# Second mixture of experts: every batch scatters its tokens to the experts' places itself, and an expert reads its places with one plain transfer

## The chip, the core and the metric

The kernel runs on one core of a Trainium2 chip. The core has five engines that run on their own and wait for each other through semaphores: PE (TensorE, matrix products and transposes), DVE (VectorE, elementwise work and reductions), ACT (ScalarE, activation functions and copies), POOL (GpSimd, elementwise work and the indirect transfers) and SP (SyncE, which issues the plain transfers). Transfers between DRAM and the on-chip memory run on 16 DMA engines. The metric is the time of one execution on the device in microseconds (us); lower is better.

## The reference, cut to what matters

Four layers of cross-attention and a feed-forward part work on `x`, 4 batches of 512 tokens of 128 numbers, in float32. All eight parts are residual: `x = x + part(layernorm(x))`. The change is in the feed-forward part of the third layer, a mixture of 8 experts of which every token uses two:

```python
logits = xf @ w_g                                  # 2048 tokens x 8 experts
topv, topi = jax.lax.top_k(logits, 2)
probs = softmax over the two
capacity = int(2 * 1.25 * 2048 / 8)                # 640 places for each expert
mask = one_hot(topi.T, 8)                          # first choices of all tokens, then second ones
rank = cumsum(mask.reshape(2 * 2048, 8), axis=0).reshape(2, 2048, 8) - 1
mask = mask * (rank < capacity)
...
h = gelu(einsum("ecd,edh->ech", exp_batches, c_fc))      # 640 x 128 by 128 x 512
exp_out = einsum("ech,ehd->ecd", h, c_proj)              # 640 x 512 by 512 x 128
out = einsum("nec,ecd->nd", cb, exp_out)                 # weighted with probs
```

First choices have precedence: a token's second choice is ranked behind the first choices of all 2048 tokens. A choice that finds no place is dropped.

## The kernel before

Tokens lie on the 128 partitions: batch `g` is a tile `X[g]` of 128 partitions by 4 (`NJ`) by 128 numbers, so there are 16 (`NT`) tiles of 128 tokens. The text is written with generators that yield between steps; `together` (L117) runs several of them in turn, one step each. A framework then puts the instructions on the engines' queues in an order of its own and adds the semaphore waits, also those for buffers that are used again. Each engine works through its queue in order.

The parts that matter here, in order of time:

- The second layer's feed-forward part `l1_ffn` (L923) ends with `write(g)` (L1053) for each batch: POOL makes masked keys (`block_keys`, L262), PE folds them (L1056), and attention over 16 slots follows. It is queued, batch by batch, with `after(g)`, the third layer's attention `attend2(g)` and `route2(g)`; `together` runs all four batches in step (L1064).
- `attend_few` (L430) is that attention. It scales the softmax terms on POOL (L449).
- `routed` (L558) normalises a batch into a tile `xn` (L230), stores it to the DRAM table `xd2` (L567, SP), transposes it on PE with some filler matmuls ahead (L89, `ident` by `ident`, results unused), and multiplies with the router's weights (L571). DVE copies the logits (L577).
- `l2_ffn` (L1090) starts when all logits are there. DVE finds both choices of all tokens (`argmax`, L586). `places` (L604) turns them into ranks with matrix products. `tokens_of_slots` (L627) turns "which place has this token" into "which token has this place" (L644 to L683): comparisons on DVE (L644, L655), 32 matmuls (L659), and a few small operations give `inv`, the token of each place, and `to`, the row of the result table `yd2` to which each place's result goes. Both are 128 by 5 (`NCH2`) by 8 experts.
- The experts: each has 640 places, that is five chunks of 128, treated as a group of three and a group of two (L1111). For each chunk POOL issues an indirect gather of 128 rows from `xd2` (L765), 40 in all. PE transposes a group (L797), DVE copies it (`exT`, L798), PE multiplies with the first weights (L1125), ACT applies gelu (L1128), PE multiplies with the second weights (L1133), DVE copies the result (`ye`, L1140), and POOL scatters it to `yd2`, one indirect transfer for each chunk (L774), 40 in all. Gathers and scatters share POOL's queue. Between the experts the weights of the fourth layer's attention are prepared (L315, L334, L349, L291).
- `combine` (L1148): SP reads `yd2` plainly (L1153), and DVE adds both choices' results, weighted, to `x` (L1159). It needs all scatters. The fourth layer follows.

The first mixture (L802) has gathers and scatters of the same kind, 8 of each, on the same two lines.

The expert weights `f2w1` and `f2w2` (L1335, L1336) are fetched during `l1_ffn`. The result table's first 4096 rows are set to zero early on (L1276), by eight SP transfers.

Of the kernel before, what the change touches and what calls it, by code (L numbers as in the profile page):

```python
# [16 lines left out]
P = 128  # L17
# [30 lines left out]
        ("tile", 2 * NT), ("row", 1), ("spare0", NEXP), ("spare2", NCH2 * NEXP), ("chunks", NCH2), ("ctxT", 128)]  # L48
# [19 lines left out]
def tile_kernel(ctx: ExitStack, tc: tile.TileContext, I, out):  # L68
# [146 lines left out]
    def normed(src, tag, plus=0.0, act=False, p=P, n=NJ, bufs=B, pool=wk):  # L215

        mv, r = yield from moments(src, p, n)
        y = pool.tile([P, n, D], F32, tag=tag, name=tag, bufs=bufs)
# [211 lines left out]
    def attend_few(g, keys, vw, H, scores_bias):  # L430
# [18 lines left out]
        nc.gpsimd.tensor_tensor(e3, e3, bc(rec, 2, M), ALU.mult)  # L449
# [108 lines left out]
    def routed(tag, w, bias=None, copies=(), fill=0):  # L558
# [5 lines left out]
        def chain(g):  # L564
            xn[g] = yield from normed(X[g], "xn")
# [38 lines left out]
    def places(ohs):  # L604

        sums, found = [], []
        for k, oh in enumerate(ohs):
            oh2 = oh.rearrange("p t e -> p (t e)")
            pt = psum()
            nc.tensor.matmul(pt[:, :P], lhsT=oh2, rhs=ones, start=True, stop=True)  # L610
            cs = rt.tile([P, P], BF16, tag="cs", name="cs", bufs=2)
            nc.scalar.copy(cs, pt[:, :P])
            sums.append(cs)
            pt = psum()
            nc.tensor.matmul(pt[:, :P], lhsT=tri, rhs=oh2, start=True, stop=False)
            for k0 in range(k):
                nc.tensor.matmul(pt[:, :P], lhsT=sums[k0], rhs=same, start=False, stop=False)
            nc.tensor.matmul(pt[:, :P], lhsT=cs, rhs=before, start=False, stop=True)
            own = rt.tile([P, NT, NEXP], F32, tag="own", name="own")
            nc.vector.tensor_tensor(own.rearrange("p t e -> p (t e)"), oh2, pt[:, :P], ALU.mult)  # L620
            rank = rt.tile([P, NT], F32, tag="rank", name="rank", bufs=2)
            nc.vector.tensor_reduce(rank, own, AX.X, ALU.add)
            nc.vector.tensor_scalar(rank, rank, -1.0, None, ALU.add)
            found.append(rank)
        return found

    def tokens_of_slots(ohs, ranks, cap, spare):  # L627

        nch = cap // P
        pt = psum()
        for k, (oh, rank) in enumerate(zip(ohs, ranks)):
            ri = rt.tile([P, NT], I32, tag="ri", name="ri", bufs=2)
            nc.vector.tensor_copy(ri, rank)
            nc.vector.tensor_scalar(ri, ri, P - 1, None, ALU.bitwise_and)
            lo = rt.tile([P, NT], BF16, tag="lo", name="lo", bufs=2)
            nc.vector.tensor_copy(lo, ri)  # L640
            Rs = []
            for t0 in range(0, NT, NJ):
                R = wk.tile([P, NJ, P], BF16, tag="aT", name="R", bufs=B)
                nc.vector.tensor_tensor(R, bc(iota, 1, NJ), bc(lo[:, t0 : t0 + NJ], 2, P), ALU.is_equal)  # L644
                Rs.append(R)
                if t0 == 0:
                    hi = rt.tile([P, NT], F32, tag="hi", name="hi", bufs=2)
                    nc.vector.tensor_tensor(hi, rank, lo, ALU.subtract)
                    in_ = rt.tile([P, NT, nch], BF16, tag="in", name="in_", bufs=2)
                    nc.vector.tensor_tensor(in_, bc(hi, 2, nch), bc(C["chunks"][:, :nch], 1, NT), ALU.is_equal)  # L650
                    tk = rt.tile([P, NT, 2, NEXP], BF16, tag="tk", name="tk", bufs=2)
                    nc.vector.tensor_scalar(tk[:, :, 0, :], oh, C["row"], None, ALU.mult)
                    nc.vector.tensor_tensor(tk[:, :, 1, :], oh, bc(C["tile"][:, k * NT : (k + 1) * NT], 2, NEXP), ALU.mult)
                    th = rt.tile([P, NT, nch, 2 * NEXP], BF16, tag="th", name="th", bufs=2)
                    nc.vector.tensor_tensor(  # L655
                        th, bc(tk.rearrange("p t i e -> p t (i e)"), 2, nch), bc(in_, 3, 2 * NEXP), ALU.mult
                    )
            for t in range(NT):
                nc.tensor.matmul(  # L659
                    pt[:, : nch * 2 * NEXP],  # L660
                    lhsT=Rs[t // NJ][:, t % NJ, :],
                    rhs=th[:, t].rearrange("p c e -> p (c e)"),
                    start=k == 0 and t == 0,
                    stop=k == len(ohs) - 1 and t == NT - 1,
                )
        inv = rt.tile([P, nch, NEXP], I32, tag="inv", name="inv")
        got = rt.tile([P, nch, 2, NEXP], F32, tag="got", name="got")
        nc.vector.tensor_copy(got.rearrange("p c i e -> p (c i e)"), pt[:, : nch * 2 * NEXP])
        token = rt.tile([P, nch, NEXP], F32, tag="token", name="token")
        nc.vector.scalar_tensor_tensor(token, got[:, :, 1, :], float(P), got[:, :, 0, :], ALU.mult, ALU.add)  # L670
        row = rt.tile([P, nch, NEXP], F32, tag="row", name="row")
        nc.vector.tensor_scalar(row, token, -1.0, 0.0, ALU.add, ALU.max)
        if len(ohs) > 1:
            again = rt.tile([P, nch, NEXP], F32, tag="again", name="again")
            nc.vector.tensor_scalar(again, row, float(NTOK), float(-NTOK), ALU.is_ge, ALU.mult)
            nc.vector.tensor_tensor(inv, row, again, ALU.add)
        else:
            nc.vector.tensor_copy(inv, row)
        to = rt.tile([P, nch, NEXP], I32, tag="to", name="to")
        none = rt.tile([P, nch, NEXP], F32, tag="none", name="none")  # L680
        nc.vector.tensor_scalar(none, token, 0.0, None, ALU.is_equal)
        nc.vector.tensor_tensor(none, none, spare.rearrange("p (c e) -> p c e", c=nch), ALU.mult)
        nc.vector.tensor_tensor(to, row, none, ALU.add)  # L683
        return inv, to
# [183 lines left out]
    def l1_xattn(keys, vw):  # L868
        def chain(g):

            def scores_bias(dst, src, r):
                for j in range(NJ):
                    s = slice(j * 2 * M, (j + 1) * 2 * M)
                    nc.vector.scalar_tensor_tensor(
                        dst[:, s].rearrange("p (h n) -> p h n", h=2),
                        src[:, j, :].rearrange("p (h n) -> p h n", h=2),
                        r[:, j : j + 1],
                        bc(bias1[:, g * NJ + j, :], 1, 2),
                        ALU.mult,
                        ALU.add,  # L880
                    )

            return attend_few(g, keys, vw, 2, scores_bias)

        return chain
# [37 lines left out]
    def l1_ffn(lw, dq, dv, cq, gw, before, after):  # L923
        sc = 1.0 / math.sqrt(8.0)
        slot_rows = lw.tile([P, 3, D], F32, tag="srows", name="slot_rows")
        e_rows = lw.tile([SEXP, 1024 + D], F32, tag="erows", name="e_rows")
        oT_all = lw.tile([P, P], F32, tag="oTall", name="oT_all")
        hM = lw.tile([P, 4 * 144], F32, tag="hM", name="hM")
        ugM = lw.tile([P, 16 * 144], F32, tag="ugM", name="ugM")
# [4 lines left out]
        def read(g):  # L934
# [3 lines left out]
            ax = lw.tile([P, 2 * P], F32, tag="ax", name="ax", bufs=B)  # L938
# [23 lines left out]
            own = lw.tile([P, 16, SLOTS], F32, tag="own", name="own")  # L962
# [25 lines left out]
        o = lw.tile([P, 1, D], F32, tag="o", name="o")  # L988
# [45 lines left out]
        nc.vector.tensor_tensor(o[:, 0, :], pt[:, :D], o[:, 0, :], ALU.add)  # L1034
        pt = psum()
# [28 lines left out]
        together(queue(write(g), after(g)) for g in range(B))  # L1064
# [12 lines left out]
    def l2_xattn(keys, vw):  # L1077
        def chain(g):
# [6 lines left out]
            return attend_few(g, keys, vw, 1, scores_bias)  # L1085
# [4 lines left out]
    def l2_ffn(xd, yd, L, f2w1, f2w2, meanwhile):  # L1090
        m1, oh1 = argmax(L)
        m2, oh2 = argmax(without(L, oh1))
        ranks = places([oh1, oh2])

        d = rt.tile([P, NT], F32, tag="d", name="d")
        nc.gpsimd.tensor_tensor(d, m2, m1, ALU.subtract)
        nc.scalar.activation(d, d, AF.Exp)
        inv, to = tokens_of_slots([oh1, oh2], ranks, L2_CAP, C["spare2"])
        wt = [rk.tile([P, NT], F32, tag=f"wt{k}", name=f"wt{k}") for k in range(2)]
        nc.vector.tensor_scalar(wt[0], d, 1.0, None, ALU.add)  # L1100
        nc.vector.reciprocal(wt[0], wt[0])
        nc.vector.tensor_tensor(wt[1], wt[0], d, ALU.mult)
# [6 lines left out]
        put = scatters(yd, to)  # L1109
# [4 lines left out]
        for i, (e, c0, m) in enumerate(groups):  # L1114
            if c0 == 0 and e:
                next(others, None)
# [406 lines left out]
```

## Time and profile before

| what | value | where from |
|---|---|---|
| median of 6 runs | 676.07 us (672.55 to 679.67) | the times |
| the profiled execution | 672.77 us, span 671.0 us | the times, the page |
| granted PE clock, mean | 0.912 of full speed | the times |
| PE busy | 534.4 us (80%) in 3443 matmuls | the page, part 1 |
| DVE, ACT, POOL busy | 330.3, 236.4, 163.4 us | the page, part 1 |
| L765 gathers, 48 | 46.1 us of POOL, 961 ns each | the page, part 5 |
| L774 scatters, 48 | 47.1 us of POOL, 981 ns each | the page, part 5 |
| L1133, L1125 matmuls | 45.0 and 39.9 us of PE | the page, part 5 |
| chain that ended last | PE 50%, DVE 5%, POOL 5%, DMA 5%, ACT 4% | the page, part 4 |

The span is the stretch from the first to the last recorded event; the time includes what lies around it. A busy share is an average over stages with different limits. In part 5 a line reads: line, engine, operation, what is written and read, how often, then busy time, mean duration, and the idle time of the engine just ahead of it with what ended most of it.

### The profile page before, as it was taken

How to read it: one execution, taken by the hardware profiler on the slowest of the kernel's cores; microseconds unless marked ns; L12 is line 12 of the kernel's file. 1: busy time of each engine (PE TensorE's matmuls, PEld its weight loads, DVE VectorE, ACT ScalarE, POOL GpSimd, SP SyncE). 2: the span in 40 equal slices, each digit the busy share in tenths (PEclk: the TensorE clock that was granted, in tenths of full speed). 3: DMA queues.
4: the chain of work that ended last, by engine and by line, in shares of the span. 5: the costliest groups of instructions: out<-in, count | busy, mean ns of one | idle time of the engine just before them, and what ended most of it. 6: DMA issues, size and time to landing. Idle time of an engine off the chain costs nothing.

```text
span 671.0 us, 9536 instructions
## 1 busy us (share of the span) xinstructions
PE 534.4 (80%) x3443; PEld 424.3 (63%) x3443; DVE 330.3 (49%) x1316; ACT 236.4 (35%) x533; POOL 163.4 (24%) x203
## 2 busy tenths in 40 slices
PE   3668988438898897899434787995499999999996
PEld 2557766328886646798413666784367967767665
DVE  4686556454387523687630221120977873333332
ACT  2354655402147423332200221322365443333332
POOL 4234234335112002000047566643110000000000
PEclk9979989858899999997758797999599999999999
DMA  8900001221791055001111112204400000000000
GB/s 324 313 26 18 16 17 48 64 86 42 253 343 47 0 182 196 2 1 31 33 27 56 33 46 47 48 28 162 121 0 1 1 1 1 17 0 17 1 17 16
DMA packets 42992, 45.01 MB, mean 67 GB/s; under 512 B 5161, under 2 KB 31026, under 8 KB 42818
## 3 DMA queue, kind: packets, MB, share of 16 engines
q1 hardware_dynamic: 39442, 36.20, 16.4%
q0 software_dynamic: 3072, 6.30, 3.5%
q10 hardware_dynamic: 432, 1.92, 0.7%
q8 instruction: 27, 0.44, 0.3%
q14 instruction: 19, 0.16, 0.1%
HBM read 34.97 MB, written 9.44 MB: 66 GB/s over the span
## 4 chain that ended last, share of the span: by engine, by line
PE 50%; DVE 5%; issue 5%; POOL 5%; DMA 5%; ACT 4%; another core or an unknown queue 3%; SPq 1%; DVEq 0%; POOLq 0%; ACTq 0%
PE pt L1250 9%; PE pt L1202 8%; PE pt L89 5%; PE pt L1125 4%; PE pt L1133 3%; POOL yd L774 3%; PE pt L392 3%; PE po L411 3%; PE pt L240 3%; PE pt L252 2%; PE pt L1004 2%; DMA yd<-ye,to 2%; PE pt L571 1%; DMA e_wg<-in_e_wg 1%
## 5 line engine op out<-in xcount | busy, mean ns | idle before, releaser
L1250 PEld LDWEIGHTS pt<-f3w,hT 128*128 128x128 f32 x512 | 65.3, 191 | 33.2 <-ACT hT L1203 18.6
L1260 DVE SCALAR_TENSOR_TENSOR x<-pt,gates,x 128x128 f32<-128x128 f32 x128 | 35.9, 344 | 77.0 <-PE pt L1250 76.8
L1203 ACT ACTIVATE hT<-pt,cols 128x512 f32<-128x512 f32 x64 | 44.0, 687 | 73.5 <-PE pt L1202 73.0
L1250 PE MATMUL pt<-f3w,hT 128*128 128x128 f32 x512 | 68.5, 277 | 1.0 <-ACT hT L1203 0.6
L1202 PE MATMUL pt<-xnT,f3w 128*128 128x512 f32 x128 | 65.1, 597 | 0.0
L1128 ACT ACTIVATE hT<-pt 128x384 f32<-128x384 f32 (+1 forms) x64 | 26.6, 439 | 102.3 <-PE pt L1125 40.5
L1133 PE MATMUL pt<-f2w,hT 128*128 128x128 f32 x320 | 45.0, 296 | 21.1 <-ACT hT L1128 15.3
L1133 PEld LDWEIGHTS pt<-f2w,hT 128*128 128x128 f32 x320 | 42.7, 205 | 26.4 <-ACT hT L1128 16.3
L765 POOL DMA_INDIRECT xg<-xd,inv x48 | 46.1, 961 | 44.8 <-DVE to L683 14.1
L89 PE MATMUL pt<-cst 128*128 128x128 f32 x392 | 56.1, 293 | 0.0
L774 POOL DMA_INDIRECT yd<-ye,to x48 | 47.1, 981 | 34.2 <-DVE ye L1140 15.6
L89 PEld LDWEIGHTS pt<-cst 128*128 128x128 f32 x392 | 52.2, 208 | 2.9 <-issue 1.7
L1140 DVE COPY ye<-pt 128x384 f32<-128x384 f32 (+1 forms) x16 | 7.9, 491 | 82.1 <-PE pt L1133 31.2
L242 ACT COPY xnT<-pt 128x512 f32<-128x512 f32 x40 | 23.4, 585 | 58.8 <-PE pt L240 58.6
L199 DVE BATCH_NORM_STATS2 st<-x 128x6 f32<-128x128 f32 x128 | 32.0, 269 | 22.3 <-POOL x L552 16.1
L240 PE MATMUL pt<-cst,xn 128*128 128x128 f32 x96 | 21.3, 310 | 25.3 <-ACT xn L226 18.1
L1125 PE MATMUL pt<-exT,f2w 128*128 128x256 f32 (+1 forms) x128 | 39.9, 455 | 0.0
L240 PEld LDWEIGHTS pt<-cst,xn 128*128 128x128 f32 x96 | 13.8, 153 | 32.1 <-ACT xn L226 20.9
L1125 PEld LDWEIGHTS pt<-exT,f2w 128*128 128x128 f32 x128 | 24.4, 203 | 8.1 <-issue 1.5
L405 PE MATMUL pt<-cst,att 128*128 128x128 f32 x128 | 20.4, 282 | 11.4 <-ACT att L379 11.4
L379 ACT ACTIVATE att<-att 128x512 f32<-128x512 f32 x32 | 20.0, 631 | 25.1 <-DVE att L378 25.0
L411 PEld LDWEIGHTS po<-v,aT 128*128 128x128 f32 x192 | 24.3, 196 | 4.5 <-issue 3.0
(327 smaller groups left out, 1031.8 us busy)
## 6 DMA issues: line engine op xcount, KB each, us to landing
e_w<-in_e_w SPq DMA_DIRECT2D x8, 512.0 KB, 7.1
e_wg<-in_e_wg SPq DMA_DIRECT2D x8, 512.0 KB, 6.5
yg<-yd SPq DMA_DIRECT2D x12, 256.0 KB, 3.7
f0w<-in_f_w SPq DMA_DIRECT2D x1, 2048.0 KB, 13.1
yd<-zero SPq DMA_DIRECT2D x8, 256.0 KB, 3.4
ew<-in_e_w SPq DMA_DIRECT2D x8, 256.0 KB, 2.7
xd<-xn SPq DMA_DIRECT2D x8, 256.0 KB, 2.2
f2w<-in_f_w SPq DMA_DIRECT2D x1, 2048.0 KB, 8.5
```

Of the source, the lines that this page charges most:

```text
L89: nc.tensor.matmul(pt[:, :P], lhsT=ident, rhs=ident, start=True, stop=True)
L199: nc.vector.bn_stats(st[:p, j, :], src[:, j, :])
L240: nc.tensor.transpose(pt[:, j * P : (j + 1) * P], src[:, j, :], ident)
L411: nc.tensor.matmul(po[:, k, :], lhsT=aT[:, k * P : (k + 1) * P], rhs=of(values[k % nch], cols + hpc, g), start=True, stop=True,)
L765: nc.gpsimd.indirect_dma_start(out=dst, out_offset=None, in_=table[:], in_offset=bass.IndirectOffsetOnAxis(ap=idx, axis=0))
L774: ins = nc.gpsimd.indirect_dma_start(out=table[:], out_offset=bass.IndirectOffsetOnAxis(ap=to[:, c, e : e + 1], axis=0), in_=y, in_offset=None
L1125: nc.tensor.matmul(pt[:, : m * P], lhsT=f2w1[:, e, f * P : (f + 1) * P], rhs=xT, start=True, stop=True)
L1133: nc.tensor.matmul(pt[:, c * D : (c + 1) * D], lhsT=hT[:, f, c * P : (c + 1) * P], rhs=f2w2[:, e, f, :], start=f == 0, stop=f == 3,)
L1202: nc.tensor.matmul(pt, lhsT=f3w1[:, e, f * P : (f + 1) * P], rhs=xnT[g], start=True, stop=True)
L1203: nc.scalar.activation(hT[:, f, :], pt, AF.Gelu, bias=col["f3_b1"][:, 2 * e + f : 2 * e + f + 1])
L1250: nc.tensor.matmul(pt[:, j, :], lhsT=hT[:, f, j * P : (j + 1) * P], rhs=f3w2[:, e, f, :], start=f == 0, stop=f == 1,)
L1260: nc.vector.scalar_tensor_tensor(xj, pt[:, j, :], ge, xj, ALU.mult, ALU.add)
```

## The change

**Sending instead of looking up.** `places` and `tokens_of_slots` go. A new function `dispatch` works on one batch at a time, queued behind its `route2(g)`. It finds both choices, and with the counts of the batches before it (`counts`) the ranks of its own tokens. First choices fill an expert's 640 places from the front, second choices from the back; a place that is claimed twice belongs to the first choice, and later batches overwrite earlier ones where that is due. So it knows the row of each of its tokens in a new table `xs2`, and POOL scatters the normalised rows there: eight indirect transfers for each batch (two choices by four tiles of 128 tokens), 32 in all. Each is made to wait for the eight transfers of the batch before.

**Numbers behind.** A row of `xs2` has 129 numbers: the 128 of the token, and the token's own number behind them. The table's 5120 places are filled early on from a new input `empty` (2.64 MB), with a number that leads to a spare row of `yd2`.

**Plain reads.** An expert's 640 rows are read by SP with one plain transfer (`xg`, 128 partitions by 5 by 129), four buffers, in place of five gathers. The last column gives the rows to which the results go: `back` says for each place whether it holds a second choice. The 40 scatters of results stay as they are.

**What goes with it.** The four `xd2` stores go. New constants `cst2` (128 by 245 numbers) are fetched where `l1_ffn`'s first buffers were, once these are free; the other constants shrink by 61 columns. The third layer's attention scales its softmax terms on DVE and no longer on POOL; the second layer's stays on POOL. The batches run in step as before (`together` with skew 0, its default).

```diff
-    def attend_few(g, keys, vw, H, scores_bias):
+    def attend_few(g, keys, vw, H, scores_bias, engine):
...
-        nc.gpsimd.tensor_tensor(e3, e3, bc(rec, 2, M), ALU.mult)
+        engine.tensor_tensor(e3, e3, bc(rec, 2, M), ALU.mult)
...
-            xn[g] = yield from normed(X[g], "xn")
+            xn[g] = yield from normed(X[g], "xn", into=rows and rows[g][:, :, :D])
...
+    def dispatch(dp, C2, xs, rows, logits, wt):
+        same3, before3 = (dp.tile([P, 96], BF16, tag=n, name=n) for n in ("b_same3", "b_before3"))
+        nc.gpsimd.tensor_copy(same3, C2["same3"])
+        nc.gpsimd.tensor_copy(before3, C2["before3"])
...
+        def own(cols, name, dtype=F32):
+            return dp.tile([P] + cols, dtype, tag=name, name=name, bufs=2)
+
+        def chain(g):
+            ts = slice(g * NJ, (g + 1) * NJ)
+            L = logits[:, ts, :]
+            nc.gpsimd.tensor_copy(rows[g][:, :, D], C2["token"][:, ts])
+            ohs = own([3, n, NEXP], "ohs", BF16)
+            w = own([2, n], "w")
+            for k in range(2):
+                nc.vector.tensor_reduce(m[:, k, ts], L, AX.X, ALU.max)
+                at = own([n, NEXP], "at", BF16)
+                nc.vector.tensor_tensor(at, L, bc(m[:, k, ts], 2, NEXP), ALU.is_equal)
+                nc.vector.tensor_tensor(at, at, bc(rev, 1, n), ALU.mult)
+                nc.vector.tensor_reduce(w[:, k, :], at, AX.X, ALU.max)
+                oh = ohs[:, 1 - k]
+                nc.vector.tensor_tensor(oh, at, bc(w[:, k, :], 2, NEXP), ALU.is_equal)
...
+            nc.scalar.copy(ohs[:, 2], ohs[:, 0])
+            while len(counts) < g:
+                yield
...
+            nc.tensor.matmul(pt[: 2 * width, :P], lhsT=flat3[:, : 2 * width], rhs=ones, start=True, stop=True)
+            cs = dp.tile([P, P], BF16, tag="cs", name="cs", bufs=B)
+            nc.scalar.copy(cs[: 2 * width], pt[: 2 * width, :P])
+            yield
+            pt = psum()[:, : 3 * width]
+            nc.tensor.matmul(pt, lhsT=tri, rhs=flat3, start=True, stop=False)
+            for c in counts:
+                nc.tensor.matmul(pt, lhsT=c[: 2 * width], rhs=same3[: 2 * width], start=False, stop=False)
+            nc.tensor.matmul(pt, lhsT=cs[: 2 * width], rhs=before3[: 2 * width], start=False, stop=True)
+            counts.append(cs)
...
+            to = own([2, n], "to", I32)
...
+            yield
+            puts = []
+            for k in range(2):
+                for j in range(NJ):
+                    ins = nc.gpsimd.indirect_dma_start(
+                        out=xs[:],
+                        out_offset=bass.IndirectOffsetOnAxis(ap=to[:, k, j : j + 1], axis=0),
+                        in_=rows[g][:, j, :],
+                        in_offset=None,
+                    ).ins
...
+                    for other in earlier:
+                        tc.add_manual_dep(
+                            ins,
+                            other.name,
+                            mybir.DependencyInfo(mybir.DependencyClass.Sync, mybir.DependencyReason.DATA),
+                            reason="rows are overwritten in the batches' order",
+                        )
+                    puts.append(ins)
+            earlier[:] = puts
+            yield
...
-        together(queue(write(g), after(g)) for g in range(B))
+        together((queue(write(g), after(g)) for g in range(B)), 0)
...
-    def l2_ffn(xd, yd, L, f2w1, f2w2, meanwhile):
+    def l2_ffn(xs, yd, back, wt, f2w1, f2w2, meanwhile):
...
+        def read(e):
+            xg.append(ex.tile([P, NCH2, D + 1], F32, tag="xg", name="xg", bufs=4))
+            nc.sync.dma_start(xg[e], xs[e * L2_CAP : (e + 1) * L2_CAP].rearrange("(p c) d -> p c d", c=NCH2))
...
-        got = [fetched(xd, inv, *group, 14) for group in groups[:3]]
-        xTs = [expert_inputs(got[0], 3)]
+        for e in range(3):
+            read(e)
+        xTs = [inputs(*groups[0])]
...
+                if e + 3 < NEXP:
+                    read(e + 3)
+                to = ex.tile([P, NCH2], I32, tag="to", name="to", bufs=NEXP)
+                nc.vector.scalar_tensor_tensor(to, back[:, e, :], float(NTOK), xg[e][:, :, D], ALU.mult, ALU.add)
...
+    nc.sync.dma_start(xs2[:NSLOT], I["empty"])
```

## The prediction

> **What bounds the kernel now.** I read the page first, then a table of windows, then the chain of waits around the second mixture, then the timelines of PE and POOL there.
>
> The page's slices, 16.8 us each:
>
> ```profile
> span 671.0 us, 9536 instructions
> ...
> PE   3668988438898897899434787995499999999996
> ...
> PEclk9979989858899999997758797999599999999999
> ```
>
> PE is nearly full except in two places, slices 8 and 9 and slices 20 to 23. The second one, about 325 to 385 us, is the routing of the second mixture (L1090), the work that the change replaces. Windows (busy us and instructions of PE, PEld, DVE, ACT, POOL, then granted clock, DMA share, GB/s):
>
> ```profile
> 320.00:330.00 10.00, 6.13 (x48) 5.06 (x48) 6.11 (x32) 2.96 (x7) 0.40 (x1) 0.86 0.12 35
> 330.00:340.00 10.00, 2.48 (x32) 2.21 (x32) 9.15 (x22) 0.83 (x1) 0.00 (x0) 0.50 0.00 0
> 340.00:350.00 10.00, 1.90 (x5) 1.08 (x6) 1.71 (x9) 0.00 (x0) 6.20 (x7) 0.50 0.20 33
> 350.00:360.00 10.00, 9.71 (x44) 6.70 (x43) 0.98 (x2) 1.97 (x4) 7.56 (x9) 0.77 0.20 54
> 360.00:370.00 10.00, 0.00 (x0) 0.00 (x0) 0.00 (x0) 0.00 (x0) 7.18 (x8) 0.74 0.18 53
> ```
>
> First DVE works alone (330 to 340: L644 and L655), then POOL issues gathers alone (L765). The chain there:
>
> ```profile
> 338.70 1.24 PE pt L659 x16
> ...
> 345.84 3.53 DMA xg<-xd,inv
> ...
> 355.50 17.13 another core or an unknown queue
> ```
>
> The last router logits are copied at 324.80 and the third gathered chunk is transposed at 347.15: 22.4 us. Then comes a hole of 17.13 us in which ACT (L1128) and DVE (L1140) wait for something that the profile cannot name, while POOL goes on issuing gathers until 369.3. A smaller one (ACT 7.63 us, DVE 9.10 us) ends at 413. From 427.76 on there are no gathers, only scatters, and PE runs almost without a break:
>
> ```profile
> 447.85 0.49 PE L797 MATMUL pt<-cst,xg 128*128 128x128 f32 x3
> 448.17 1.89 PE L1125 MATMUL pt<-exT,f2w 128*128 128x256 f32 x8
> 449.90 2.02 PE L1133 MATMUL pt<-f2w,hT 128*128 128x128 f32 x16
> 451.76 0.38 PE L797 MATMUL pt<-cst,xg 128*128 128x128 f32 x2
> 451.98 2.75 PE L1125 MATMUL pt<-exT,f2w 128*128 128x384 f32 x8
> 454.56 3.02 PE L1133 MATMUL pt<-f2w,hT 128*128 128x128 f32 x24
> 457.41 1.89 PE L1125 MATMUL pt<-exT,f2w 128*128 128x256 f32 x8
> ```
>
> One expert takes 457.41 - 447.85 = 9.56 us here, against 14.5 (398.45 to 412.92, ye to ye) while POOL issues ten transfers for an expert. POOL's spacing and the landing of its last scatter:
>
> ```profile
> 462.27 0.97 POOL L774 DMA_INDIRECT yd<-ye,to  x1 [0.30 <-issue]
> 463.55 0.97 POOL L774 DMA_INDIRECT yd<-ye,to  x1 [0.31 <-issue]
> ```
>
> ```profile
> 463.55 4.62 DMA yd<-ye,to
> 468.19 2.63 DMA yg<-yd
> ```
>
> So one indirect transfer costs POOL 1.28 us from start to start; the last scatter's landing lets SP go 4.62 us after it began; the first plain read lands 2.63 us later. Between the last logits and 468.19 this stage takes 143.4 us.
>
> **The change, part by part.** I follow the same stretch, to the landing of the last `yd` scatter, because what is after it is not touched.
>
> *Ahead of the router.* `cst2` (123 KB) is fetched into memory that is free only after the add of L1034 (253.93). Six small POOL copies wait for it and stand ahead of the third and fourth batch's `keys` (L262, 257.39). POOL ends `keys` two at 257.14; a landing in 2.2 us (the `xd` stores' median) after 254.3 is about then, so the six copies (nearest rows 0.17 to 0.55 us, L300 and L340, overlapping) cost about 0.9 us; bounds 0 and 3. `f2w1` stands behind `cst2` on SP and starts about 0.3 us later; 2 MB in 8.5 us are needed at 391, so hidden; without that cover 0.3. The softmax scaling L449 goes from POOL (0.41 and 0.13 of hand-over) to DVE (four times 0.29 by L1083): DVE is full from 295.8 to 302.9, but PE's fillers (L89, 6.89 us from 311.40) stand behind; I take 0.3, bounds -0.5 and 1.2. The copy of 2.64 MB of empty slots sits on SP behind the eight zero stores; between 25 and 50 us the DMA engines are 36% busy, and its data is needed past 330. At 347 GB/s, the rate of the first 25 us, both directions would be 15 us after 32.5, all hidden: SP's next transfer (L981) was let go at 56.6; with no cover, 15. The four `xd2` stores go; they landed in 2.2 us, long before the gathers: nothing. First logits: 321.26 + 0.9 + 0.3 = 322.5.
>
> *Argmax and places, by batch.* The compiled order keeps the four batches in step through the router. From the first logits to the first batch's row numbers DVE issues four `rows` normalisations (0.26 each, L230) and 32 small operations. The 24 small ones from 325.20 to 330.11 came every 0.205 us; these are smaller, I take 0.19. 1.05 + 6.1 + about 0.6 for the hop through ACT and PE gives 330.2; POOL starts 0.85 later, as after L676 (341.12 to 341.97): **331**; bounds 329 and 333. The other batches' work lies under the first one's scatters.
>
> *32 scatters in place of 40 gathers.* POOL's order shows that the first scatter of each batch waits for all eight landings of the batch before. One batch: 7 x 1.28 + 4.62 + 0.85 = 14.4 us. Four: 331 + 3 x 14.4 + 8.96 + 4.62 = **387.8**. Rows are 516 bytes and not 512; no row shows that. Landing bounds: 2.56 (gather begun 344.59, transposed 347.15) and 5.84 (the first mixture's last scatter). I take 4.62: same kind, same destination. Behind the waiting scatter stand only later scatters. On DVE the third batch's row numbers wait for the first batch's landing (two buffers), with the fourth's and the experts' behind them: about 344.5, before POOL wants them. On ACT the gelu table (1.28) waits for the scatters' landing, in the shade of the read.
>
> The Trainium skill (DMA: Bandwidth & Descriptors, Anatomy of one DMA) fits a POOL-issued transfer as about 2.0 us plus bytes over 436 GB/s. That makes 2.15 us of landing, four times 2.47 less, and a time near 685; the row of 4.62 decides. The same section warns that completion into HBM can be surprisingly long, which speaks against a chain of four of them.
>
> *Plain reads.* 330 KB instead of 256: 2.63 to 3.4 us (scaled by size), I take 3.1 and 0.2 to PE: first data at **391.1**. The other reads follow at once and are refilled after an expert's transposes, 5 us before they are wanted.
>
> *The experts.* First expert on a cold PE (clock 0.50 in 350 to 354): three transposes of 0.45, a copy 0.56 with gaps, L1125 at half clock 1.51 + 3.72, a last activation 0.6, then 2.85 + 0.33 + 1.73 + 1.86 by the chain: 14.6 us. Seven more at 9.56: 66.9. Key preparation in between, four L315 of 0.87, L334 0.89, L349 and L291 0.86: 5.2. Bubbles: the expert before the quoted one took 11.15, 0.7 more than 9.56 + 0.89; four of these, 2.8. Sum 89.5, and from the last L1133 to the landing 461.0 to 468.19 = 7.2. POOL has five scatters, 6.4 us, per expert: no bound. End: 391.1 + 96.7 = **487.8** against 468.2.
>
> So +19.6 us: span 690.6, profiled time 672.77 + 19.6 = 692.4. The median of the six runs is 3.3 above the profiled execution, so I say **695**. What goes away (the 40 gathers and the holes beside them) is worth about 25 us of expert loop; what comes is a wait of some 45 us more ahead of the first expert.
>
> **The rivals.**
>
> 1. *The hole is not the gathers'.* It could belong to the first matmuls after a pause or to code loading: then 13 us of it (359.70 to 372.6) return, 708. For: ACT and DVE wait for PE, whose records end at 359.7. Against: both holes fall where POOL issues gathers, and none after them. Part of it could recur beside the plain reads.
> 2. *Scatters land like gathers, 2.56 us.* Four times 2.06 less: 687. For: the same bytes. Against: both scatter rows, 4.62 and 5.84.
> 3. *The other side: the batches overlap.* If the waits between batches did not bind and the first batch sent while the others were still in attention, the scatters would be over when the last batch is. Place: POOL's queue between 311 and 388. Each us by which the last scatter lands earlier is a us; it decides at 20 us, a landing at 368. Waits alone gone are worth 3 x 5.47 = 16.4, 679; with a start at 321 (logits without the small operations) 669. For: the operations are written by batch. Against: the compiled order has all four batches' normalisations (L230) ahead of the first argmax, and the eight waits stand there.
> 4. *The rows in DRAM do not do what the text says*, as with a scatter broken into 512 and 4 bytes, twice the descriptors: 1.28 becomes up to 2.2 and 32 x 0.9 = 29 are added, 724. No row shows 516 bytes.
>
> **How the numbers follow.** Forecast 0.62, rival 1 0.17, rival 2 0.12, rival 3 0.06, rival 4 0.03. Low end: start 329.5, landings 2.56, loop 2.7 less, read 2.65: about 683. High end: start 333, landings 5.84, read 4.0, loop 3.3 more: about 707, and up to 712 for part of rival 1. Range 683 to 712. A change under 0.5% (3.4 us) cannot be told from none here. Faster 0.04 and the same 0.03 come from rival 3 and the edge of rival 2; slower 0.93.
>
> **What would show it.** In the profile after: POOL with four groups of eight `xs` scatters, start to start about 14.4 us; PE idle from about 330 to 391; `xg` issued near 388; no hole of over 5 us in the expert loop; an expert every 9.6 to 11 us; the last `yd` scatter landing near 488. I am wrong if the groups are closer than 12 us, if the first begins before 325, or if PE stalls again within the first two experts.

## The result, and the profile after

The changed kernel takes 679.97 us (median of 21 runs, 676.25 to 683.35), the kernel before 675.81 (47 runs beside them, 672.55 to 679.67): a ratio of 1.0054, 95% interval 1.004 to 1.0069. It is slower, as predicted, but by 4 us and not by 19 (695 had been forecast, with 683 as the low end of the range). The profiled execution took 681.44 us, with a span of 679.6.

The page's slices of the changed kernel, 17.0 us each:

```profile
span 679.6 us, 9549 instructions
...
PE   3668988439898897899500499995399999999996
...
PEclk9878989858899999896755699998599999999999
```

The gap of PE is deeper, slices 20 to 23 (5, 0, 0, 4 in place of 4, 3, 4, 7), and the four behind it are full (9, 9, 9, 9 in place of 8, 7, 9, 9). The windows there (same columns as before):

```profile
330.00:340.00 10.00, 3.39 (x22) 1.79 (x22) 6.86 (x57) 2.00 (x9) 5.63 (x6) 0.61 0.10 33
340.00:350.00 10.00, 0.00 (x0) 0.00 (x0) 0.23 (x2) 0.00 (x0) 5.99 (x8) 0.50 0.13 40
350.00:360.00 10.00, 0.00 (x0) 0.00 (x0) 0.23 (x2) 0.00 (x0) 6.39 (x7) 0.50 0.15 48
360.00:370.00 10.00, 0.00 (x0) 0.00 (x0) 0.00 (x0) 0.00 (x0) 6.08 (x7) 0.50 0.12 40
```

From 340 on POOL works alone, and the DMA engines are nearly idle (12 to 15%). Its timeline at the border between the first two batches of scatters (start, us, idle before and what ended it), and from the chain of waits the landings (start of the transfer, us until it lets its successor go):

```profile
341.79 0.96 POOL L679 DMA_INDIRECT xs<-rows,to  x1 [0.30 <-issue]
344.93 0.96 POOL L679 DMA_INDIRECT xs<-rows,to  x1 [2.18 <-DVE to L672]
```

```profile
341.79 2.37 DMA xs<-rows,to
...
377.59 2.28 DMA xs<-rows,to
380.26 2.67 DMA xg<-xs
...
469.99 5.50 DMA yd<-ye,to
```

A batch's last scatter lands 2.37 us after its start, and the next batch begins 3.14 us after that start. The four batches begin 12.08, 11.90 and 11.91 us apart: forecast were 14.4, and under 12 was the prediction's own sign of being wrong. (The POOL line names DVE's `to`, L672, as what ended the wait; `own_rows` below shows that it is not.) The last scatter of `yd`, the same kind of transfer, takes 5.50 us. PE in the expert loop:

```profile
383.06 1.30 PE L829 MATMUL pt<-cst,xg 128*128 128x128 f32 x5 [45.39 <-DMA xg<-xs]
...
426.26 1.02 PE L319 MATMUL pt<-keys,fa 128*128 128x512 f32 x2
427.12 0.38 PE L829 MATMUL pt<-cst,xg 128*128 128x128 f32 x2
...
436.69 1.02 PE L319 MATMUL pt<-keys,fa 128*128 128x512 f32 x2
437.55 0.38 PE L829 MATMUL pt<-cst,xg 128*128 128x128 f32 x2
```

An expert takes 437.55 - 427.12 = 10.43 us, without a hole.

### The profile page after: what moved, and what is told of

Its sections match the earlier page's. It is cut to its first block, busy times and chain, and to the rows that moved or that the text cites. A ratio compares the mean times of both kernels' runs of the same rounds, so it can differ in the third digit from the quotient of the medians.

```text
span 679.6 us, 9549 instructions
## 1 busy us (share of the span) xinstructions
PE 532.2 (78%) x3426; PEld 424.4 (62%) x3426; DVE 325.9 (48%) x1353; ACT 238.8 (35%) x539; POOL 155.0 (23%) x196
## 4 chain that ended last, share of the span: by engine, by line
PE 26%; issue 18%; POOL 8%; DMA 5%; ACT 2%; DVE 2%; POOLq 0%; DVEq 0%; SPq 0%
PE pt L1298 9%; PE pt L1250 8%; POOL yd L1182 6%; DMA xs<-rows,to 3%; POOL xs L679 2%; PE pt L396 2%; PE po L415 2%; PE pt L256 1%; PE pt L93 1%; PE pt L244 1%; DMA yd<-ye,to 1%; ACT xnT L246 1%; PE pt L575 1%; PE pt L1165 1%; DVE x L1207 1%
## 5 line engine op out<-in xcount | busy, mean ns | idle before, releaser
L93 PE MATMUL pt<-cst 128*128 128x128 f32 x392 | 56.8, 295 | 0.0
L1182 POOL DMA_INDIRECT yd<-ye,to x40 | 39.5, 989 | 52.9 <-DVE ye L1180 29.8
L829 PE MATMUL pt<-cst,xg 128*128 128x128 f32 x48 | 10.4, 307 | 51.7 <-DMA xg<-xs 45.4
L679 POOL DMA_INDIRECT xs<-rows,to x32 | 30.8, 963 | 86.7 <-issue 77.6
L1173 PEld LDWEIGHTS pt<-f2w,hT 128*128 128x128 f32 x320 | 39.6, 191 | 4.0 <-ACT hT L1168 0.9
L1173 PE MATMUL pt<-f2w,hT 128*128 128x128 f32 x320 | 40.8, 280 | 0.4 <-ACT hT L1168 0.4
L829 PEld LDWEIGHTS pt<-cst,xg 128*128 128x128 f32 x48 | 6.7, 155 | 54.8 <-issue 51.8
L244 PE MATMUL pt<-cst,xn 128*128 128x128 f32 x80 | 18.1, 323 | 26.1 <-ACT xn L230 18.9
L1165 PE MATMUL pt<-exT,f2w 128*128 128x256 f32 (+1 forms) x128 | 38.3, 443 | 0.2 <-DVE exT L830 0.2
L244 PEld LDWEIGHTS pt<-cst,xn 128*128 128x128 f32 x80 | 12.0, 159 | 32.7 <-ACT xn L230 21.7
L396 PE MATMUL pt<-keys,xnT 128*128 128x256 f32 (+1 forms) x64 | 28.4, 555 | 1.3 <-ACT xnT L246 1.3
L1165 PEld LDWEIGHTS pt<-exT,f2w 128*128 128x128 f32 x128 | 23.7, 195 | 8.7 <-issue 0.9
## 6 DMA issues: line engine op xcount, KB each, us to landing
xg<-xs SPq DMA_DIRECT2D x8, 322.5 KB, 4.1
```

The costliest lines, as they stand in the source:

```text
L93: nc.tensor.matmul(pt[:, :P], lhsT=ident, rhs=ident, start=True, stop=True)
L244: nc.tensor.transpose(pt[:, j * P : (j + 1) * P], src[:, j, :], ident)
L396: nc.tensor.matmul(pt[:, j * nk : (j + 1) * nk], lhsT=xT[:, (j0 + j) * P : (j0 + j + 1) * P], rhs=keys, start=True, stop=True,)
L679: ins = nc.gpsimd.indirect_dma_start(out=xs[:], out_offset=bass.IndirectOffsetOnAxis(ap=to[:, k, j : j + 1], axis=0), in_=rows[g][:, j, :] ...
L1165: nc.tensor.matmul(pt[:, : m * P], lhsT=f2w1[:, e, f * P : (f + 1) * P], rhs=xT, start=True, stop=True)
L1173: nc.tensor.matmul(pt[:, c * D : (c + 1) * D], lhsT=hT[:, f, c * P : (c + 1) * P], rhs=f2w2[:, e, f, :], start=f == 0, stop=f == 3,)
```

## The experiments

In every session the kernel before ran beside the experiments, and so it turned out that its own time is not the same everywhere: 676 us in the runs shown above, whose chip is not on record, 678 and 679 in two sessions on chip 0, 651 to 652 on chips 2, 9 and 14. Each of these three ran in one session only, so that it is the chip, and not the session, is likely and not shown. Every time below is given with its chip.

### How long a scatter takes to land

`late_fetch` (chip 2) moves the fetch of the expert weights beside the scatters:

```diff
-    nc.sync.dma_start(f2w1, ...)
-    nc.sync.dma_start(f2w2, ...)
+    for ins in (nc.sync.dma_start(f2w1, ...).ins, nc.sync.dma_start(f2w2, ...).ins):
+        tc.add_manual_dep(ins, first_scatter.name, ...)
```

> The changed kernel with the fetch of f2w1 and f2w2 (2 MB each, plain, SP) let go only by the first batch's first scatter, near 333 us, so that it lies beside the first scatters. Theory A (a scatter's landing is 2.4 us where the DMA engines are free and about 5 where a plain fetch of megabytes is under way; the last yd scatter meets the fetch of f3w): while the fetch lasts, about 12 us, the landing of the last scatter of the first batch is 4.5 to 6, the second batch starts 2 to 3.5 us later, the third perhaps as well; time +2 to +6. Rival B (the long landings belong to the yd table or to five scatters of one expert, not to the fetch): landings stay at 2.4, the groups 11.9 apart, the time within 1 us.

Landings in its chain of waits, and the windows of the fetch:

```profile
342.95 6.03 DMA xs<-rows,to
...
353.55 2.27 DMA xs<-rows,to
```

```profile
341.00:345.00 4.00, 0.00 (x0) 0.00 (x0) 0.00 (x0) 0.00 (x0) 2.30 (x3) 0.50 1.04 397
345.00:349.00 4.00, 0.00 (x0) 0.00 (x0) 0.00 (x0) 0.00 (x0) 0.00 (x0) 0.50 1.04 372
```

The one landing of this chain that met the fetch (DMA share 1.04) took 6.03 us; those behind it took 2.27 to 2.35. The second batch began 15.75 us after the first in place of 12.08 (3.7 later, a little more than theory A said), the later ones 11.9 apart. From the first scatter's start to the last landing it is 50.7 us against 47.0 (377.59 + 2.28 - 332.85), and the median is 682.27 (679.97 above). Theory A holds.

`no_f3_fetch` (chip 2) takes away the fetch beside the last `yd` scatter:

```diff
-        f3w1 = moe.tile([P, NEXP, 256], F32, tag="w1", name="f3w1")
-        f3w2 = moe.tile([P, NEXP, 2, D], F32, tag="w2", name="f3w2")
+        f3w1 = f2w1[:, :, :256]
+        f3w2 = f2w2[:, :, :2, :]
...
-                nc.sync.dma_start(f3w1, ...)
-                nc.sync.dma_start(f3w2, ...)
```

> The changed kernel without the fetch of the fourth layer's expert weights (f3w1, f3w2, 2 MB): its experts use parts of f2w1 and f2w2 that lie there already, so the fourth layer's mixture computes with other weights; the amount of PE work is the same. Theory A (the last yd scatter lands 5.5 us after its start because that fetch runs beside it): it lands in 2.3 to 2.7 us, and the first read of yd2 follows 3 us earlier. Rival B (the yd table or the number of scatters in flight): it stays at 4.5 to 5.8 us.

```profile
467.07 2.22 DMA yd<-ye,to
```

5.50 became 2.22 us (chain of waits): theory A again. On the same chip, with the fetch, `own_rows` and `skew4` have 5.20 and 5.48 there. The row that the prediction took as "the same kind" was a scatter beside 2 MB of plain traffic.

### The wait between batches

`own_rows` (chip 2) gives every batch rows of its own:

```diff
-    xs2 = dram.tile([SPARE + 2 * NTOK, D + 1], ...)
+    xs2 = dram.tile([B * (SPARE + 2 * NTOK), D + 1], ...)
...
-                        tc.add_manual_dep(ins, other.name, ...)
+                        tc.declare_no_dep(ins, other, ...)
```

> The changed kernel with rows of its own in xs2 for every batch, so that no batch waits for another; the experts read the first batch's rows alone, so the tokens of the other three batches are left out of the mixture's result, and the amount of work is the same. Theory A (the wait between the batches is the landing of the last scatter, 2.4 us, and 0.8 to restart, less the 1.27 that a scatter takes anyway): start to start 1.27 throughout, the last scatter starts 31 x 1.266 = 39.2 us after the first in place of 44.7, the time falls by 5.6 us to about 674.4. Rival B (the wait is covered by something else, as DVE's row numbers, which stand at the same moment): the groups stay 11.9 us apart and the time stays at 680.

From its POOL timeline, the last scatter of the first batch and the first of the second:

```profile
342.36 0.96 POOL L679 DMA_INDIRECT xs<-rows,to  x1 [0.30 <-issue]
343.62 0.96 POOL L679 DMA_INDIRECT xs<-rows,to  x1 [0.30 <-issue]
```

The scatters run through at 1.27 us, the last starts 39.27 us after the first (333.43 to 372.70), and the median is 673.76. The three waits cost 44.74 - 39.27 = 5.5 us together, as theory A said. DVE's `to` of the third batch still comes late here, at 344.76, when the second batch's scatters have been running since 343.62: it holds nothing up, and rival B falls.

### The holes of the kernel before

`plain_chunks` replaces the 40 gathers by plain reads, `eight_bufs` gives the gathers 8 buffers, `before_again` and `before_third` are the kernel before:

```diff
-            gather(xs[-1], xd, inv[:, c, e : e + 1])
+            nc.sync.dma_start(xs[-1], xd[at : at + P])      # plain_chunks
...
-                got.append(fetched(xd, inv, *groups[i + 3], 14))
+                got.append(fetched(xd, inv, *groups[i + 3], 8))      # eight_bufs
```

> The kernel before, unchanged, profiled once more, because its runs beside the last four experiments took 651 us (648.9 to 652.9) and those shown with the prediction 676. Theory A (the 24.5 us are the two holes beside the gathers, 355.5 to 372.6 and the one that ends at 413, and they are not in every session): this profile shows an expert loop without a hole of over 5 us and a total near 651, with the stages ahead of the loop and behind it as before; or, where the total is 676 again, the holes are there again. Rival B: the 24.5 us are spread over the whole span, as a higher clock would do it (0.92 against 0.91 cannot), and the holes are there in both.

> The kernel before with 8 buffers for gathered chunks in the second mixture in place of 14. Theory A (PE's transposes of a group are held until the last gather that POOL issued ahead has landed, so the hole is as long as the row of gathers issued ahead): where before shows its hole, it gets shorter by about six gathers, 7 us, and before's 676 becomes 669; where before shows none, nothing changes (within 2 us). Rival B (the hole has nothing to do with how many are ahead): the same time as before, or later, as gathers now wait for buffers.

> The kernel before with the 40 gathers of the second mixture replaced by 40 plain reads of 128 rows in a row from xd2, issued by SP, so that the experts work on tokens that the router did not choose; everything else stays, the making of the rows too. Theory A (the holes come with POOL's gathers): no hole of over 5 us, the first expert at once behind the row numbers, an expert every 9.6 to 11 us; loop about 85 us, total 645 or less. Rival B (the holes belong to the first matmuls after a pause or to code loading): a hole of 13 to 17 us after the first group again.

On chip 9 `before_again` took 650.83 us, theory A's case. The same activation (L1128) in the first profile of before, and in `before_again` (ACT's timelines, idle time in brackets):

```profile
372.61 1.21 ACT L1128 ACTIVATE hT<-pt 128x256 f32<-128x256 f32 x4 [17.11 <-remote]
```

```profile
358.65 1.68 ACT L1128 ACTIVATE hT<-pt 128x256 f32<-128x256 f32 x4 [2.95 <-PE pt L1125]
```

POOL issues the same 22 gathers in a row, 1.25 us apart, in both. In the second nothing stands still (windows of `before_again`):

```profile
350.00:360.00 10.00, 10.00 (x48) 7.35 (x48) 1.54 (x3) 3.16 (x8) 7.56 (x9) 0.76 0.21 54
360.00:370.00 10.00, 10.00 (x68) 8.64 (x67) 3.44 (x8) 3.47 (x9) 7.57 (x9) 1.00 0.21 53
```

Ahead of 358 us the two profiles agree within 0.3 us, so the 24.5 us lie in the loop. 14 of them are the first hole: of its 17.11 us, 2.95 are an ordinary wait, and DVE's first `ye` (L1140) comes at 358.22 in place of 372.57. Another 12 lie in the four experts behind it, three of which take 14.5 us each (10.4 to 12.0 here); one of the three has the second hole, in the other two the profile names PE as what ended the wait, so there the hole is argued and not shown. Some 4 us come back behind the loop. Code loading does not tell the two profiles apart: from 358 to 372.6 us each brings in one packet of code. Without the holes `eight_bufs` (chip 9) had nothing to win (654.13 against 651.39). `plain_chunks` took 635.22 in its one run there, with full windows from 340 on.

> The kernel before, unchanged, in one more session. Theory A (the two holes of the first profile, 17.1 and 9.1 us, are a property of the chip or of the session): 651 without holes or 676 with them, nothing between, and PE, ACT and DVE stand still together in the holes. Rival B (they come and go from one execution to the next): some runs at 651, some at 660 to 676.

> The kernel before with 8 buffers for gathered chunks in place of 14, once more. Where before shows its holes here (676): theory A, that a hole lasts as long as POOL issues gathers without a pause, makes it shorter by six gathers, to about 669; rival B leaves 676 or more. Where before shows none (651), it is 654 again, and the holes stay open.

> The kernel before with 40 plain reads in place of the 40 gathers, once more; the experts work on tokens that the router did not choose. Where before takes 677: theory A (the holes come with POOL's gathers) says no hole of over 5 us and 633 to 642 as in the first run; rival B (that chip stops PE, ACT and DVE in this stretch whatever POOL does) says holes of 9 us or more and 655 or more. Where before takes 651 it says nothing new.

Chip 0 has the holes: `before_third` 677.67, all eight runs between 676 and 679 (theory A: they do not come and go), first hole 17.48 us on ACT. `eight_bufs_2` shows that the first hole follows the row of gathers; its ACT and POOL timelines:

```profile
369.68 1.21 ACT L1128 ACTIVATE hT<-pt 128x256 f32<-128x256 f32 x4 [9.24 <-remote]
```

```profile
365.80 0.95 POOL L765 DMA_INDIRECT xg<-xd,inv  x1 [0.30 <-issue]
370.47 0.99 POOL L774 DMA_INDIRECT yd<-ye,to  x1 [3.73 <-DVE ye L1140]
```

16 gathers in a row and 9.24 us, in place of 22 and 17.48: 8.2 us less for six gathers. The total did not follow (677.21, ratio 0.998, 0.995 to 1.0009), and four more holes of 6.3 to 7.0 us came later in place of one of 7.8: theory A was right on the hole and wrong on the time. With plain reads the same chip shows no hole of over 5 us, and 640.12 us (ratio 0.9426, 0.9389 to 0.9463). The holes come with rows of POOL's gathers; whether with their issue on POOL or with their traffic is not told apart, and on chips 2, 9 and 14 no profile shows one.

> The changed kernel, unchanged, on the same chip as before_again. Theory A (it has no gathers in the second mixture and so no such holes): 680 again, whatever the kernel before does; the change then costs about 28 us where the holes of before are absent and 4 where they are there. Rival B (a session in which everything is faster): 655.

On chip 9 the changed kernel took 676.16 (ratio 1.0424, 1.0367 to 1.0481): it has no holes to lose, and the change costs 25 us there.

### Batches out of step

`skew4` and `skew8` set the last argument of `together` to 4 and 8; `before_skew4` does so in the kernel before; `late_empty` moves the copy of the empty places behind the fetch of the new constants; `skew6_late_empty` has both:

```diff
-        together((queue(write(g), after(g)) for g in range(B)), 0)
+        together((queue(write(g), after(g)) for g in range(B)), 4)
...
-    nc.sync.dma_start(xs2[:NSLOT], I["empty"])
...
             C2 = packed("cst2", _CST2, pool=dp)
+            tc.add_manual_dep(nc.sync.dma_start(xs2[:NSLOT], I["empty"]).ins, fetches[-1].name, ...)
```

> The changed kernel with its batches four steps apart instead of in step from L1112 on; nothing else differs and the output is the reference's. Theory A (the stage is a chain of four batches of scatters, 11.9 to 12.1 us each, and only the last batch has to stand behind the last logits): the first scatters start while the other batches are still in attention, before 320 us; behind the last logits lie about 6.7 us of row numbers, 8.9 of scatters and 2.4 of landing in place of 6.7 + 36 + 8.9 + 2.4. Up to 36 us go; if the attention, with fewer batches side by side, ends some 8 us later, the time is about 652. Rival B (what lies between 260 and 325 us is full because the batches are in step): the last logits come 30 us or more later, and the time is 672 or more.

> The kernel before with its batches four steps apart from L1064 on. Its row numbers need the logits of all batches, so nothing of the routing can start early. Theory A (the 9 to 13 us that skew4 gained came from scatters under the attention): here the last logits come later (342.6 in skew4 against 329.8), and the time is 8 to 14 us longer than before's. Rival B (out of step is better for the attention itself): no longer, or shorter.

> The changed kernel with its batches eight steps apart. Theory A (the end is the later of two chains: the first scatter plus 47.3 us, which is 31 x 1.27, three restarts of 1.8 and 2.3 of landing, or the last batch's logits plus some 8 + 8.9 + 2.3 = 19 us): the first batch's logits come by about 300, so its chain would end by 355; the last logits come by about 350 and decide, the last scatter lands near 369, time within 4 us of skew4's 667. Rival B (the attention loses nothing more by being further apart): last logits at 343 as in skew4, last landing 362, time 662.

> The changed kernel with the copy of the 2.64 MB of empty places let go only behind the fetch of the new constants, near 265 us, in place of 33; nothing else differs. Theory A (that copy, beside the first layer's loads, is what moves the start of the second normalisation, L234 first xn, from 97.2-97.6 in four profiles of the kernel before to 97.2-100.3 in five of the changed one): xn begins at 97.2 to 97.7, the first router logits are copied at 322 to 323, and the median falls by about 2 us. Rival B (the delay is the lower granted clock of those executions, whatever its cause, and the copy has no part in it): xn begins anywhere in 97 to 100 again and the median stays.

> The changed kernel with its batches six steps apart and the copy of the empty places behind the fetch of the new constants. Theory A: both chains of the last text meet near the last landing of 363 to 365, and the first layer runs as in the kernel before: 660 to 665, better than the changed kernel by 15 and than 676, but not better than the 651 of the kernel before where that has no holes. Rival B (the copy near 265 us meets the weights' fetch and delays the first scatter): 667 or more.

| kernel (chip) | last logits | first scatter | last scatter | median, us |
|---|---|---|---|---|
| changed, in step (9) | 326.0 | 329.1 | 373.7 | 676.16 |
| `skew4` (2) | 342.6 | 319.3 | 364.4 | 666.79 |
| `skew8` (14) | 352.5 | 306.7 | 367.0 | 670.76 |
| `skew6_late_empty` (14) | 347.8 | 308.4 | 362.2 | 664.48 |
| `before_skew4` (14) | 339.2 | - | - | 666.94 |

`skew4` gains 9 us against the changed kernel on chip 9 (651 for the kernel before on both chips), and not the 24 of its theory A, for two reasons: the last logits come 13 us later than in the profile after (329.8), not 8, and the four batches of scatters still follow each other for 47.3 us from the first one, which started at 319.3 only. `skew8` gets an early start and pays with late logits, as theory A said. `skew6_late_empty` came where its theory A put it (660 to 665). `before_skew4` loses 15 us against 651.96 (8 to 14 expected), so the gain is the scatters' and not the attention's. `late_empty` (chip 14) went to rival B: `xn` began at 99.8 all the same, at a granted clock of 0.84 from 50 to 70 us, and the median stayed at 679.84; so the copy in the first layer costs nothing that these runs can show.

> The version six steps apart with the late copy of the empty places, once more, to see it beside a kernel before that has its holes. Theory A (it has no gathers, so it does not depend on whether a chip shows the holes): 662 to 667 wherever it runs, so that it is 2% faster than before where before takes 677 and 2% slower where before takes 651. Rival B (a chip with holes stops this version as well): 675 or more where before takes 677.

On chip 0 the same version took 675.96 (ratio 0.9966, 0.9943 to 0.9988). Rival B: it has holes there too, now beside the first batch's scatters (ACT and DVE timelines, then POOL's):

```profile
320.50 0.59 ACT L248 COPY xnT<-pt 128x512 f32<-128x512 f32 x1 [5.46 <-remote]
```

```profile
320.60 0.36 DVE L426 RECIPROCAL rec<-po 128x32 f32<-128x32 f32 x1 [4.70 <-remote]
```

```profile
317.91 0.96 POOL L681 DMA_INDIRECT xs<-rows,to  x1 [0.31 <-DMA xs<-rows,to]
333.03 0.96 POOL L681 DMA_INDIRECT xs<-rows,to  x1 [14.15 <-DVE st L205]
```

Both engines are let go 2.6 to 2.7 us after the last scatter of the row began, and the last logits come 10.7 us later than on chip 14. What is sent beside attention is exposed to the holes; the changed kernel in step sends while nothing else runs. The six-step version is a third of a per cent faster than the kernel before on chip 0; where there are no holes, no version that computes the reference beats the kernel before.

## Why the prediction was right in direction and wrong in size

The prediction's terms against the profile after, in us:

| term | predicted | measured | difference |
|---|---|---|---|
| first logits | 322.5 | 326.12 | +3.6 |
| to the first scatter | 8.5 | 6.73 | -1.8 |
| first scatter's start to the last landing | 56.8 | 47.02 | -9.8 |
| to the first transpose | 3.3 | 3.19 | -0.1 |
| expert loop, to the end of the last L1173 | 89.5 | 84.43 | -5.1 |
| to the last `yd` landing | 7.2 | 8.01 | +0.8 |
| what is left of the time | 204.6 | 205.94 | +1.3 |
| sum | 692.4 | 681.44 | -11.0 |

The median missed its forecast by 15: these 11, and 4 because the prediction put the median 2.6 us above the profiled execution, as in the runs before, and it lies 1.5 below.

**The step that failed** is the landing: "Landing bounds: 2.56 ... and 5.84 ... I take 4.62: same kind, same destination." The mechanism was right, four batches each waiting for the landing of the one before; its size was off. It measured 2.3 us, four times 2.3 less, which is all but 0.5 us of the 9.8. Even the low end of the range had 2.56 for it, and a loop only 2.7 us shorter where it was 5.1. Both rows that made 4.62 look safe, the last scatters of the two mixtures, were not free transfers. In the trace of before SP issues `f3w1` and `f3w2` just ahead of the scatter at 463.55 (SP's timeline):

```profile
459.33 0.37 SPq L1347 DMA_DIRECT2D f3w<-in_f_w  x1
461.25 0.71 SPq L1348 DMA_DIRECT2D f3w<-in_f_w  x1
```

In `before_again` POOL is still scattering when that fetch is over, and the same last scatter, of the same kernel, lands in 2.23 us. Beside the first mixture's 5.84 the DMA share is 1.05 (171 to 174 us). `no_f3_fetch` and `late_fetch` show for the second mixture that the fetch makes the difference; for the first it was not tried. The nearer row was the gather at 2.56, which stood there as rival 2 (687).

By the fit of the Trainium skill (DMA: Bandwidth & Descriptors, Anatomy of one DMA) the estimate for such a transfer was 2.15 us. The runs agree where the DMA engines are free (2.22 to 2.45) and not beside a fetch (5.50 and 6.03); its warning of long completions into HBM was not what made the rows long.

**The expert loop** was 5.1 us shorter. The terms taken from rows were right: 9.56 + 0.87 = 10.43 measured 10.43. The first expert took 12.3 us (383.06 to 395.38) and not 14.6 (its first L1165 group 3.97 us in place of 5.23), and of the 2.8 us of bubbles, four times the excess of one expert of before, one pause of 0.42 us is left.

**The first logits** came 3.6 us later than predicted in this execution; in `after_again` they came at 322.36, where they were expected. Most of the difference is there long before the routing: the first `xn` (L234) starts at 99.3 us in one and at 97.2 in the other. It goes with the clock and not with the change: in eight of the eighteen profiles the granted clock is 1.00 from 50 to 70 us, and `xn` starts at 97.2 to 97.9; in the other ten it is 0.83 to 0.91, and `xn` starts at 98.2 to 100.3, a profile of the kernel before (`before_third`, 99.97) among them. What sets the clock was not tried.

**What was right:** 1.28 us from scatter to scatter (1.265 with rows of 516 bytes, so rival 4 fell), the six POOL copies (0.9), the read, the wait of all scatters of a batch for those before, no hole over 5 us, POOL no bound in the loop.

**Rival 1** (the hole is not the gathers') fell: no hole after, though the first matmuls come behind a pause of 45 us, and none with plain reads. But the prediction booked "about 25 us of expert loop" as what the change removes, without asking whether the holes are always there. They are not. So what the change costs depends on where it runs, 4 us between the medians above and 25 on chip 9, and the 19 forecast are neither. The stage on chip 9 beside the first pair of profiles:

| stretch, change from before to after | with holes | without (chip 9) |
|---|---|---|
| to the first logits | +4.9 | +1.0 |
| first logits to the transpose that starts the loop | +31.0 | +31.0 |
| expert loop, to PE's last matmul of the mixture | -29.4 | -1.8 |
| to the last `yd` landing | +0.8 | -4.2 |
| rest of the span | +1.3 | -0.3 |
| sum | +8.6 | +25.7 |

What the change costs is the same in both, 31 us of waiting for the first data. What it gives back is 29.4 us of loop where gathers cause holes, and 1.8 where they do not. The -4.2 is POOL again: without holes the loop of before ends ahead of POOL, whose scatters run on to 442.55 while PE's last matmul of the mixture ended at 433.46.

**Rival 3** (overlap) does not happen in step; made to happen, it is worth 9 to 12 us where there are no holes, not the 16 to 26 of its text. The waits alone, 16 there, are worth 5.5 (`own_rows`): the mis-sized landing again.

## What to carry to other kernels

Before a row of the trace prices a transfer, look at what else the DMA engines carry in that moment: a 128-row scatter landed in 2.3 us alone and in 5 to 6 beside a weight fetch. A hole in the kernel before whose cause the profile cannot name is not a saving to book: profile it in another session or on another chip, and give the forecast with and without it. A transfer that consumers read in pieces (gathers) hides under their work; one that must be complete before the first read (scatters) does not, and moving it ahead of the producer's end gains only as much as the producer's own overlap allows.

## What was not expected of the hardware

On chip 0, and in the first profile of before, ACT and DVE, and PE behind them, stand still for 5 to 17 us while POOL goes on issuing indirect transfers, gathers (17.48 and 9.24 us) or scatters (5.46); they go on 2.6 to 4.6 us after the start of the last transfer of the row. No profile from chips 2, 9 and 14 shows such a pause; the kernel before, profiled again on chip 9, is 25 us faster for it. The Trainium skill (SBUF — State Buffer, SBUF: two separate sides) says that PE and ACT wait at no port for another engine; the trace names no releaser ("remote"), so neither a port nor anything else is shown as the cause, and why the chips (or the sessions) differ stays open.
